# Folding a bias network's hidden rows twice by DMA, so that one last product takes 32 keys

## The chip, the core and the metric

The kernel runs on one core of a Trainium2 chip. It is one launch that computes four layers of a network, one after the other, in float32. The metric is the device time of that launch in microseconds (us). The engines have short names in the profile: PE is TensorE (matmuls) and PEld its weight loads, DVE is VectorE, ACT is ScalarE, POOL is GpSimd, SP is SyncE, which here issues DMAs. DMAs are issued by SP (plain copies) and by POOL (here all that accumulate into their target).

## The reference, cut to what matters

The change concerns layer 0 alone, an attention with a position bias that a small network computes. Per image (2) and head (8) there are 1024 queries on a 32 x 32 grid and 64 keys. For each pair of a query and a key:

```
pos  = grid_q[:, :, None, :] - grid_kv[:, None, :, :]
bias = jnp.sign(pos) * jnp.log1p(jnp.abs(pos))
bias = jax.nn.relu(bias @ cpb_w1 + cpb_b1)        # 2 -> 128
bias = jax.nn.relu(bias @ cpb_w2 + cpb_b2)        # 128 -> 128
bias = (bias @ cpb_w3 + cpb_b3)                   # 128 -> 1
sim  = q k^T + bias;  attn = softmax(sim);  out = attn v
```

The 128 x 128 product in the middle runs for 2 x 8 x 64 x 1024 pairs, about a million. Afterwards come a projection, a residual and an MLP, and then layers 1 to 3, which are further attentions on the same activations.

## The kernel before, in words

**Tiling of the bias network.** A unit u is one of the 16 (image, head) pairs. Its 64 keys are worked on in 16 quads of four keys; a quad is named by u, o (0 to 7) and half (0 or 1), and the loop in `layer0` runs over all 256 quads in this order. `first_hidden` lets DVE write the first hidden layer of the next quad: per key a tile of 128 channels x 1024 queries. `second_hidden` multiplies it, in four parts q of 32 output channels (line 704). In each part the four keys stand at four groups of 32 PSUM rows, so that four matmuls of 32 columns each run side by side; a quad has 32 matmuls, and the trace shows two records for each. ACT adds the bias, applies the ReLU and moves each part to an SBUF tile y (line 709).

**The sum over channels.** The last product, with `cpb_w3`, is a weighted sum over the 128 channels. `sorted_weights` has pulled the magnitude of each weight into the channel, and sorted the channels by the sign of the weight, so that rows which are to be added have one sign. The sum is then made of additions:

- part 0 is multiplied by a sign for each row (ACT, line 711), and added to part 1 by an accumulating DMA that POOL issues (L716);
- part 2 is added to part 3 by POOL (L720);
- one quad later, `join` adds part 1 to part 3 (POOL, L723). What remains of a quad is one tile with 32 rows for each of four keys;
- after the second quad of a pair, `join` issues two more accumulating DMAs on POOL, each 64 rows of 1024 numbers: in each of the two tiles, every second row is added to its neighbour (L725 and L726); a plain copy on SP (L727) puts the second tile's rows into the free rows of the first. Now one tile has 8 keys with 16 rows each.

**The last product.** `last_product` (L742) takes two such tiles, of 16 keys in all: four matmuls, one for each tile and each half of the queries, each with a matrix of 32 columns (`folded`) that adds up a key's 16 rows with their sign and places the key in `sim`. It stands in PE's queue four quads after the last quad of its 16 keys. When a unit's last product is done, `attend` adds the query-key product to `sim` (L768) and runs the softmax, one step a quad.

**What sets the order.** The order of PE, ACT, DVE and POOL is written out by hand (`manual_schedule`): each engine works its instructions in the order in which the loop emits them. SP works its DMAs in order as well, and waits ahead of each for what it needs. Two lists of generators, `front` (offsets, sampling and the log tables of units to come) and `after` (attention and projection of units done), are advanced by a step a quad. On SP and POOL stand also the table loads of `first_hidden`: once in four quads SP loads log positions (L620) and POOL turns them into a table tx (L622), which the first hidden layer of later quads needs. The tiles y have 2, 3, 2 and 6 buffers (tags h20 to h23).

Of the kernel before, what the change touches and what calls it, by code (L numbers as in the profile page):

```python
# [11 lines left out]
F32 = mybir.dt.float32  # L12
AF = mybir.ActivationFunctionType
ALU = mybir.AluOpType
AX = mybir.AxisListType
# [3 lines left out]
P = 128  # L19
B, C, H, W = 2, 512, 32, 32  # L20
N = H * W
CT = C // P
NB = N // P
HF = 512
DH = 64
NJ = 64
# [9 lines left out]
    ("index", 1), ("row", 1), ("sixes", 16),  # L36
# [12 lines left out]
N_FOLDED, N_SINGLE = 56, 60  # L49
# [7 lines left out]
class Net:  # L57
# [40 lines left out]
    def layer0(self):  # L98


        nc, io = self.nc, self.io
        with ExitStack() as ctx:
            keep = self.pool(ctx, "l0")
            self.l0qkv = keep.tile([P, 3, CT, P], F32, tag="qkv", name="qkv")
            x_in = io["x"].rearrange("b (t p) h w -> b t p (h w)", p=P)
            nc.scalar.dma_start(self.cols, io["cols"])
            for bt in range(BP):
                b, t = divmod(bt, CT)
# [4 lines left out]
            self.l0w2 = keep.tile([P, P], F32, tag="w2", name="w2")  # L113
# [8 lines left out]
            ow = keep.tile([P, CT, C], F32, tag="ow", name="ow")  # L122
# [8 lines left out]
            self.hid2 = self.pool(ctx, "c_hid2", 1)  # L131
            self.soft = self.pool(ctx, "c_soft", 1)
            apool = self.pool(ctx, "c_att", 1)
            ps = self.ps_h = self.pool(ctx, "c_ps_h", 3, psum=True)
# [11 lines left out]
            with self.tc.manual_schedule(engines=engines):  # L146
# [23 lines left out]
                pairs[0]["xT"] = self.fone.tile([P, NB, P], F32, tag="xnT", name="xnT00")  # L170
# [15 lines left out]
                held, self.join, self.first_z = [], None, None  # L186
                batch = []
                for i, (u, o, half) in enumerate(quads):
                    self.half = half
                    if o == 1 and half == 1 and u % 2 == 0 and u // 2 + 1 < BP:  # L190
                        nxt = pairs[u // 2 + 1]
                        front += [self.offsets(nxt, u // 2 + 1, ps), self.sampled(nxt, u // 2 + 1, ps)]
                    h1 = ready
                    if i + 1 < len(quads):
                        if quads[i + 1][1:] == (7, 0) and u + 1 < 2 * BP:
                            self.advance(front, lambda: "logs" in pairs[(u + 1) // 2])
                        ready = self.first_hidden(*quads[i + 1], pairs, tables)
                    z = self.second_hidden(u, o, half, h1, i + 1 == len(quads))
                    if half == 0:
                        batch.append((o % 2, z))  # L200
                    elif o % 2 == 1:
                        held.append((u, o, batch))
                        batch = []
                        if len(held) == 2:
                            v, last, zs = held.pop(0)
                            self.last_product(v, last, zs, sims, ps_s)
                            if last == 7:
                                if v == 8:
                                    self.advance(after, lambda: False)
                                    att = [  # L210
                                        apool.tile([P, N], F32, tag=f"att{t}", name=f"att{v}_{t}") for t in range(CT)
                                    ]
                                self.advance(front, lambda: "v" in pairs[v // 2])
                                after.append(self.attend(v, pairs[v // 2], sims.pop(v), att, ps))
                                if v % 8 == 7:
                                    after.append(self.projection(ps, att, ow, v // 8))
                    if not self.step(after):
                        self.step(front)
# [3 lines left out]
                (_, _, (ready, first)), = held  # L222
                self.last_product(u, o, [ready], sims, ps_s)
                self.single_product(u, o, 0, first[1], sims)
# [4 lines left out]
                self.single_product(u, o, 1, z, sims)  # L229
# [29 lines left out]
    def sorted_weights(self, keep):  # L259
# [7 lines left out]
        self.places = keep.tile([P, P + N_FOLDED + N_SINGLE], F32, tag="places", name="places")  # L267
        nc.scalar.dma_start(self.places, self.io["places"])
        before = keep.tile([P, P], F32, tag="before", name="before")
# [3 lines left out]
        names = ("pos", "six", "rest", "late", "gap", "neg", "first", "second", "rank", "mag", "sign")  # L273
# [8 lines left out]
        many = keep.tile([P, 16], F32, tag="many", name="sort_many")  # L282
        vec.tensor_tensor(many, self.colr("sixes", 16), total.to_broadcast([P, 16]), ALU.is_le)
        vec.tensor_reduce(c["six"], many, AX.X, ALU.add)
        vec.tensor_scalar(c["late"], c["six"], 6.0, None, ALU.mult)
        vec.tensor_scalar(c["rest"], c["six"], -6.0, 96.0, ALU.mult, ALU.add)
# [14 lines left out]
        pool.tensor_scalar(c["sign"], self.col("row"), c["six"], 2.0, ALU.is_lt, ALU.mult)  # L301
        pool.tensor_scalar(c["sign"], c["sign"], -1.0, 1.0, ALU.add, ALU.mult)
        self.folded = keep.tile([P, N_FOLDED], F32, tag="folded", name="folded")
        self.single = keep.tile([P, N_SINGLE], F32, tag="single", name="single")
        pool.tensor_scalar(self.folded, self.places[:, P : P + N_FOLDED], c["sign"], 1.0, ALU.mult, ALU.mult)
        pool.tensor_scalar(self.single, self.places[:, P + N_FOLDED :], c["sign"], 1.0, ALU.mult, ALU.mult)
        yield
        perm = keep.tile([P, P], F32, tag="perm", name="perm")
# [60 lines left out]
    def offsets(self, m, bt, ps):  # L369
# [11 lines left out]
        prod = self.fone.tile([P, 6, 6, NJ], F32, tag="prod", name=f"prod{b}{t}")  # L381
# [79 lines left out]
    def first_conv(self, qp, prod, conv, ps):  # L461
# [3 lines left out]
        diag = []  # L465
        for k in range(both, len(TAPS)):
            i = (k - both) % 8
            if i == 0:
                diag.append(self.hid2.tile([P, 8, P], F32, tag="h23", bufs=6, name=f"diag{k}"))
            nc.gpsimd.tensor_scalar(diag[-1][:, i, :], self.ident, self.col("dw_w", k), 1.0, ALU.mult, ALU.mult)  # L470
# [30 lines left out]
    def normed(self, m, bt, ahead=None):  # L501
        nc = self.nc
        b, t = divmod(bt, CT)
        if ahead:
            xn = self.hid2.tile([P, N], F32, tag="h23", bufs=6, name=f"xn{b}{t}")
        else:
            xn = self.fone.tile([P, N], F32, tag="xn", name=f"xn{b}{t}")
        m["xn"] = xn
        (ahead or nc.vector).tensor_scalar(
            xn, self.xs[b][t], self.s1[:, t : t + 1], self.col("bn1_b", t), ALU.mult, ALU.add  # L510
        )
# [30 lines left out]
    def sampled(self, m, bt, ps):  # L542
# [7 lines left out]
        if "xT" not in m:  # L550
            xT = self.fone.tile([P, NB, P], F32, tag="xnT", name=f"xnT{b}{t}")
            nc.scalar.copy(xT, self.turn(m, bt, ps))
            m["xT"] = xT
# [3 lines left out]
        w = self.fone.tile([P, NB, 2 * NJ], F32, tag="w", name=f"w{b}{t}")  # L557
# [46 lines left out]
        yield  # L604

# [85 lines left out]
    def second_hidden(self, u, o, half, h1, final):  # L691
# [6 lines left out]
        for q in range(4):  # L698
# [8 lines left out]
            y = self.hid2.tile([P, N], F32, tag=f"h2{q}", bufs=(2, 3, 2, 6)[q], name=f"h2_{u}_{o}{half}{q}")  # L707
# [14 lines left out]
        def join(final, z=ys[3], other=ys[1], first=self.first_z, fold=half == 1 and not final):  # L722
            (nc.vector if final else nc.gpsimd).tensor_tensor(z, z, other, ALU.add)  # L723
            if fold:
                nc.gpsimd.dma_start(first[0::2, :], first[1::2, :], accum_op=ALU.add)  # L725
                nc.gpsimd.dma_start(z[1::2, :], z[0::2, :], accum_op=ALU.add)  # L726
                nc.sync.dma_start(first[1::2, :], z[1::2, :])  # L727

        self.join, self.first_z = join, ys[3]
        return ys[3]  # L730

    def last_product(self, u, o, zs, sims, ps_s):

        if u not in sims:
            sims[u] = ps_s.tile([P, HF], F32, tag="sim", name=f"sim{u}")
        sim = sims[u]
        at = 24 - 4 * (o - o % 2)
        for h in range(2):  # L740
            for jj, z in zs:
                self.nc.tensor.matmul(  # L742
                    sim[h * NJ + jj * 32 : h * NJ + jj * 32 + 32, :],
                    lhsT=self.folded[:, at : at + 32],
                    rhs=z[:, h * HF : (h + 1) * HF],
                    start=(o < 2),
                    stop=False,
                )
# [1240 lines left out]
def _places():  # L1989

    q, row = np.arange(P) // 32, np.arange(P) % 32
    got = np.zeros((P, P + N_FOLDED + N_SINGLE), np.float32)
    got[:, :P] = np.where(q == 0, 96 + row, 6 * (row // 2) + 2 * (q - 1) + row % 2)
    p = np.arange(P)
    got[p, P + 24 + 4 * (p % 2) + p // 32] = 1
    got[p, P + N_FOLDED + 28 + p // 32] = 1
    return got


def _layout(i):  # L2000
# [10 lines left out]
    def over(v):  # L2011
        return np.broadcast_to(v.reshape(1, -1), (P, v.size))
# [12 lines left out]
        "row": (np.arange(P) % 32 // 2).astype(np.float32).reshape(P, 1), "sixes": over(np.arange(6, 102, 6, dtype=np.float32)),  # L2025
# [46 lines left out]
```

## Time and profile before

| | |
|---|---|
| median of 3 runs | 3251.7 us (3251.33 to 3252.86) |
| profiled execution | 3251.48 us, its span 3249.7 us |
| layer 0's loop over quads | from about 30 to about 1930 us |
| PE busy, from 100 to 1900 us | 1799.6 of 1800 us |
| POOL, ACT, DVE busy, same window | 1624, 1416, 1399 us |
| share of the 16 DMA engines busy, same window | 0.68, moving 143 GB/s |
| last product (L742), same window | 488 records, 64.4 us |
| granted PE clock | full |

The page gives busy time for each engine, then the chain of work that ended last, then groups of instructions by line. A group's row holds its count, its busy time with the mean of one in ns, and the idle time of its engine just ahead of it, with what ended most of that. Ends of matmuls are modelled, and spans on POOL are rough, so where an engine is in a steady rhythm the distance between starts says more than a duration. For a DMA the row of its line has the time that the issuing engine spends; the time from issue to landing is given apart.

### The profile page before, as it was taken

How to read it: one execution, taken by the hardware profiler on the slowest of the kernel's cores; microseconds unless marked ns; L12 is line 12 of the kernel's file. 1: busy time of each engine (PE TensorE's matmuls, PEld its weight loads, DVE VectorE, ACT ScalarE, POOL GpSimd, SP SyncE). 2: the span in 40 equal slices, each digit the busy share in tenths (PEclk: the TensorE clock that was granted, in tenths of full speed). 3: DMA queues.
4: the chain of work that ended last, by engine and by line, in shares of the span. 5: the costliest groups of instructions: out<-in, count | busy, mean ns of one | idle time of the engine just before them, and what ended most of it. 6: DMA issues, size and time to landing. Idle time of an engine off the chain costs nothing.

```text
span 3249.7 us, 59022 instructions
## 1 busy us (share of the span) xinstructions
PE 3230.7 (99%) x24436; PEld 1200.2 (37%) x24436; DVE 2388.3 (73%) x2745; ACT 1960.0 (60%) x2032; POOL 2351.6 (72%) x1563
## 2 busy tenths in 40 slices
PE   9999999999999999999999999999999999999999
PEld 4333333333333333333333334444555533455333
DVE  7877878878877677878877765575465689855897
ACT  7787887887887587887887751111131466213662
POOL 7998999999998698998999973433333458634575
PEclk9999999999999999999999999999999999999999
DMA  6676776667766566676666761111000100000001
GB/s 172 144 151 136 154 148 144 144 145 146 148 147 132 104 149 137 139 153 140 147 145 144 150 163 67 52 39 39 0 1 1 40 1 1 15 1 14 1 1 53
DMA packets 96571, 309.35 MB, mean 95 GB/s; under 512 B 14688, under 2 KB 16864, under 8 KB 93216
## 3 DMA queue, kind: packets, MB, share of 16 engines
q0 software_dynamic: 57040, 200.31, 32.6%
q1 hardware_dynamic: 38240, 103.05, 9.8%
q8 instruction: 197, 3.23, 0.4%
q10 hardware_dynamic: 1008, 2.06, 0.2%
q14 instruction: 86, 0.70, 0.1%
HBM read 67.34 MB, written 4.46 MB: 22 GB/s over the span
## 4 chain that ended last, share of the span: by engine, by line
PE 80%; POOL 11%; DVE 6%; issue 2%; ACT 1%; DMA 0%; DVEq 0%; POOLq 0%; ACTq 0%; SPq 0%
PE hp L704 41%; PE s L1610 5%; PE o L1639 5%; POOL h L723 4%; POOL h L720 4%; PE qk30P L1385 1%; PE qk20P L1385 1%; PE qk21P L1385 1%; PE m_6P L899 1%; PE m_4P L899 1%; PE m_2P L899 1%; PE m_0P L899 1%; PE qk31P L1385 1%; PE m_5P L899 1%; PE m_3P L899 1%
## 5 line engine op out<-in xcount | busy, mean ns | idle before, releaser
L704 PE MATMUL hp<-h,w2s 128*32 128x512 f32 x16384 | 1784.0, 593 | 0.5 <-DVE h L680 0.2
L680 DVE CUSTOM_DVE_ANT_1 h<-tx,bank 128x1024 f32<-128x1024 f32 (+1 forms) x1028 | 1180.4, 1211 | 299.8 <-PE hp L704 238.2
L709 ACT ACTIVATE h<-hp,magb 128x1024 f32<-128x1024 f32 x1024 | 1132.6, 1110 | 379.4 <-PE hp L704 368.7
L704 PEld LDWEIGHTS hp<-h,w2s 128*32 128x32 f32 x16384 | 531.3, 110 | 1211.9 <-issue 1184.9
L720 POOL TENSOR_TENSOR h<-h,h 128x1024 f32<-128x1024 f32 x255 | 816.6, 3203 | 1.5 <-ACT h L709 1.5
L723 POOL TENSOR_TENSOR h<-h,h 128x1024 f32<-128x1024 f32 x254 | 748.5, 2947 | 1.7 <-DMA h<-h 1.6
L716 POOL DMA_DIRECT2D h<-h x255 | 302.4, 1186 | 192.3 <-ACT h L709 179.3
L1614 ACT ACTIVATE e<-s 128x1024 f32<-128x1024 f32 x256 | 261.8, 1025 | 181.0 <-PE s L1610 175.1
L711 ACT ACTIVATE h<-h,flip 128x1024 f32<-128x1024 f32 x256 | 294.4, 1150 | 8.4
L1639 PE MATMUL o<-e,v 64*64 64x512 f32 x2048 | 265.3, 590 | 2.2 <-DVE q L1678 2.2
L1610 PE MATMUL s<-q,k 64*64 64x512 f32 x2048 | 266.0, 591 | 0.0
L1621 POOL TENSOR_TENSOR some<-some,e 128x1024 f32<-128x1024 f32 x64 | 167.6, 2619 | 26.7 <-ACT e L1614 24.2
L1619 POOL TENSOR_TENSOR some<-e,e 128x1024 f32<-128x1024 f32 x32 | 76.1, 2378 | 141.3 <-DVE sum L1628 106.3
L726 POOL DMA_DIRECT2D h<-h x127 | 175.3, 1381 | 1.0 <-issue 1.0
L725 POOL DMA_DIRECT2D h<-h x127 | 148.5, 1169 | 0.0
L1626 DVE TENSOR_TENSOR sum<-sum,e 128x1024 f32<-128x1024 f32 x64 | 123.9, 1936 | 29.9 <-ACT e L1614 26.8
L869 POOL TENSOR_TENSOR mlp_w<-mlp_w 128x512 f32<-128x512 f32 x16 | 21.2, 1325 | 164.8 <-DMA mlp_w<-in_mlp_w 140.4
L1639 PEld LDWEIGHTS o<-e,v 64*64 64x64 f32 x2048 | 77.9, 133 | 144.9 <-issue 134.8
L1610 PEld LDWEIGHTS s<-q,k 64*64 64x64 f32 x2048 | 76.6, 133 | 133.1 <-issue 117.2
L960 ACT ACTIVATE mh<-mh,cols 128x512 f32<-128x512 f32 x64 | 46.1, 721 | 124.3 <-DVE mh L978 65.4
L1373 POOL TENSOR_TENSOR sq<-q 128x512 f32<-128x512 f32 x32 | 33.2, 1039 | 99.2 <-DVE q L1392 55.1
L1624 DVE TENSOR_TENSOR sum<-e,e 128x1024 f32<-128x1024 f32 x32 | 80.8, 2524 | 32.0 <-ACT e L1614 32.0
(582 smaller groups left out, 3358.6 us busy)
## 6 DMA issues: line engine op xcount, KB each, us to landing
h<-h POOLq DMA_DIRECT2D x255, 512.0 KB, 5.4
h<-h POOLq DMA_DIRECT2D x254, 256.0 KB, 5.0
h<-h SPq DMA_DIRECT2D x127, 256.0 KB, 4.0
lb<-logs SPq DMA_DIRECT2D x63, 512.0 KB, 5.8
mlp_w<-in_mlp_w SPq DMA_DIRECT2D x16, 1024.0 KB, 5.0
x<-in_x SPq DMA_DIRECT2D x8, 512.0 KB, 7.5
qkw<-in_l_qk SPq DMA_DIRECT2D x2, 2048.0 KB, 8.0
out<-x SPq DMA_DIRECT2D x15, 256.0 KB, 2.1
```

The source lines that it names most:

```text
L680: self.nc.vector._custom_dve(TENSOR_ADD_SAT, out=h1[r][:, k, cut, :], in0=x[:, 4 * half + 2 * r + k, :].unsqueeze(1).to_broadcast([P, H // ...
L704: nc.tensor.matmul(hp[rows, cut], lhsT=self.l0w2[:, 32 * q : 32 * q + 32], rhs=h1[k][:, cut], start=True, stop=True)
L709: nc.scalar.activation(y, hp, AF.Relu, bias=self.magb[:, q, 0:1])
L711: nc.scalar.activation(y, y, AF.Copy, scale=self.flip)
L716: nc.gpsimd.dma_start(y, ys[0], accum_op=ALU.add)
L720: (nc.vector if final else nc.gpsimd).tensor_tensor(y, y, ys[2], ALU.add)
L723: (nc.vector if final else nc.gpsimd).tensor_tensor(z, z, other, ALU.add)
L726: nc.gpsimd.dma_start(z[1::2, :], z[0::2, :], accum_op=ALU.add)
L899: self.nc.tensor.matmul(acc[p], lhsT=w[:, a, k, p * P : (p + 1) * P], rhs=right(r, k), start=k == 0, stop=k == 1)
L1610: nc.tensor.matmul(s[halves[c], par, :], lhsT=ks[p][rows, at : at + DH], rhs=qs[p][rows, cut], start=True, stop=True)
L1614: nc.scalar.activation(e, s, AF.Exp, scale=DH**-0.5)
L1639: nc.tensor.matmul(o[halves[par], r, :], lhsT=v[n // 2][rows, n % 2, at : at + DH], rhs=e[rows, par, :], start=(n == 0), stop=(n == NB - 1),)
```

## The change

The tiles of part 3 of both halves of a pair become one double tile `both` of 128 rows x 2 x 1024 (three buffers). The pair is folded once by a single accumulating DMA over 64 rows of 2 x 1024, in place of L725 and L726. Two quads after the pair's second quad, the new `refold` issues a second accumulating DMA on POOL, 32 rows of 2 x 1024, after which a key has 8 rows; it stands ahead of part 3's ReLU in the program, so ahead of the L720 addition of that quad on POOL. Two plain copies on SP then gather the rows of each half, 32 rows of 1024 each, in a tile `sum` (three buffers). Two `sum` tiles hold 32 keys, and `twice_product` multiplies them in four matmuls, once in eight quads, again four quads after the last quad of the set. The last eight quads of the layer keep the single fold and the products of before, for the shorter tail.

`sorted_weights` sorts the channels so that four neighbouring rows have one sign, not two (the counts `sixes` become `twelves`); its scratch tiles, and other short-lived ones, now lie in buffers of the new tags: `spare` and `diag` in `sum`, the early `xn` in `two`; the convolution's products and the sampling's weights and image share a tile `big`. Nothing else of the kernel is changed, and the new file has new line numbers: L704 becomes L729, L716 L746, L720 L750, L723 L753, L620 L645, L622 L647. The diff, cut to its core:

```diff
-                    z = self.second_hidden(u, o, half, h1, i + 1 == len(quads))
+                    last_set = i >= len(quads) - 8
                     if half == 0:
-                        batch.append((o % 2, z))
-                    elif o % 2 == 1:
-                        held.append((u, o, batch))
-                        batch = []
-                        if len(held) == 2:
-                            v, last, zs = held.pop(0)
-                            self.last_product(v, last, zs, sims, ps_s)
...
+                        if i + 2 < len(quads):
+                            both = self.two_tiles(f"h2_{u}_{o}3")
+                            group.append([both[:, 0, :], both[:, 1, :], both])
+                        else:
+                            group.append([self.four_rows(f"h2_{u}_{o}{n}3") for n in range(2)])
+                        if o % 4 < 2 and not last_set:
+                            sums.append(self.four_rows(f"sum{u}_{o}"))
+                    self.second_hidden(i, u, o, half, h1, group[-1], i + 1 == len(quads), last_set)
+                    if half == 1 and not last_set:
+                        self.refolds.append((i + 2, group[-1][2], sums[o % 2], o % 4 // 2))
+                    if half == 1 and o % 4 == 1 and summed:
+                        v, e, zs = summed
+                        self.twice_product(v, e, zs, sims, ps_s)
+                        summed = None
...
+                    elif half == 1 and o % 4 == 3:
+                        if last_set:
+                            self.folded_product(u, o - 2, group[:2], sims)
+                        else:
+                            summed, group, sums = (u, o // 4, sums), [], []
...
@@ second_hidden
-            y = self.hid2.tile([P, N], F32, tag=f"h2{q}", bufs=(2, 3, 2, 6)[q], name=f"h2_{u}_{o}{half}{q}")
+            if q < 3:
+                y = self.hid2.tile([P, N], F32, tag=f"h2{q}", bufs=(2, 3, 2)[q], name=f"h2_{u}_{o}{half}{q}")
+            else:
+                y = one[half]
+                if self.refolds and self.refolds[0][0] <= i:
+                    self.refold(*self.refolds.pop(0)[1:])
...
             if fold:
-                nc.gpsimd.dma_start(first[0::2, :], first[1::2, :], accum_op=ALU.add)
-                nc.gpsimd.dma_start(z[1::2, :], z[0::2, :], accum_op=ALU.add)
-                nc.sync.dma_start(first[1::2, :], z[1::2, :])
+                nc.gpsimd.dma_start(one[2][0::2], one[2][1::2], accum_op=ALU.add)
+                if last_set:
+                    nc.sync.dma_start(one[0][1::2, :], one[1][0::2, :])
...
+    def refold(self, both, to, second):
+        nc = self.nc
+        nc.gpsimd.dma_start(both[0::4], both[2::4], accum_op=ALU.add)
+        for half in range(2):
+            nc.sync.dma_start(to[2 * second + half :: 4, :], both[0::4, half, :])
+
+    def twice_product(self, u, e, zs, sims, ps_s):
+        if u not in sims:
+            sims[u] = ps_s.tile([P, HF], F32, tag="sim", name=f"sim{u}")
+        at = 16 - 16 * e
+        self.sum_product(u, self.twice[:, at : at + 32], e == 0, zs, sims)
...
+    def four_rows(self, name):
+        return self.hid2.tile([P, N], F32, tag="sum", bufs=3, name=name)
+
+    def two_tiles(self, name):
+        return self.hid2.tile([P, 2, N], F32, tag="two", bufs=3, name=name)
```

## The prediction

> **What bounds the kernel now.** I read the page's first part, then its chain, then the groups, and last the timeline around the products that the change touches.
>
> ```profile
> PE 3230.7 (99%) x24436; PEld 1200.2 (37%) x24436; DVE 2388.3 (73%) x2745; ACT 1960.0 (60%) x2032; POOL 2351.6 (72%) x1563
> ...
> PE 80%; POOL 11%; DVE 6%; issue 2%; ACT 1%; DMA 0%; DVEq 0%; POOLq 0%; ACTq 0%; SPq 0%
> ...
> L704 PE MATMUL hp<-h,w2s 128*32 128x512 f32 x16384 | 1784.0, 593 | 0.5 <-DVE h L680 0.2
> ...
> L720 POOL TENSOR_TENSOR h<-h,h 128x1024 f32<-128x1024 f32 x255 | 816.6, 3203 | 1.5 <-ACT h L709 1.5
> L723 POOL TENSOR_TENSOR h<-h,h 128x1024 f32<-128x1024 f32 x254 | 748.5, 2947 | 1.7 <-DMA h<-h 1.6
> L716 POOL DMA_DIRECT2D h<-h x255 | 302.4, 1186 | 192.3 <-ACT h L709 179.3
> ...
> L726 POOL DMA_DIRECT2D h<-h x127 | 175.3, 1381 | 1.0 <-issue 1.0
> L725 POOL DMA_DIRECT2D h<-h x127 | 148.5, 1169 | 0.0
> ```
>
> PE is never idle, and its 16,384 hidden-layer records waited 0.5 us in all. The 99% alone proves little, because ends of matmuls are modelled; the timeline of PE, cut to two lines, proves it:
>
> ```profile
> 607.13 13.92 PE L704 MATMUL hp<-h,w2s 128*32 128x512 f32 x128
> ...
> 634.94 1.04 PE L742 MATMUL sim<-h,folded 128*32 128x512 f32 x8
> ```
>
> 128 records (two quads) take 13.87 us wherever the chain shows them as one piece, so eight records take 13.87 x 8 / 128 = 0.867 us, without a gap. Layer 0's time is the sum of its matmuls, and a product on L742, eight records, costs 0.867 us (its shown 1.04 includes a modelled tail: the one at 606.27 was followed by the next quad at 607.13, 0.86 later).
>
> **What the Trainium skill says.** Trace Analysis (its opening note) calls matmul busy time a bad metric since matmuls are pipelined; hence the spacing above. TensorEngine Tiling, Key Properties: column tiles run independently and in parallel. The trace agrees: a record lasts 593 ns, and eight pass in 867. DMA: Bandwidth & Descriptors, Anatomy of one DMA: DMA engines do not wait on semaphores, the issuing sequencer does; so a copy that is not ready blocks everything behind it on SP. The same page, SDMA does more than copy: an accumulate handles at most 2048 elements; the new fold's rows are exactly 2 x 1024, the old ones 1024. No run here shows yet how such a row goes.
>
> **The change part by part.**
>
> *Products.* Before: 63 full products of four matmuls, and two lone matmuls of L742 at the end. After: 31 products of 32 keys, one folded product for half of the last set, and the same two lone matmuls. The two built programs' counts, 254 and 130 matmuls, agree: 124 go, that is 31 products. 31 x 0.867 = 26.9 us. All stood on PE in order, with nothing to hide them.
>
> *POOL.* Per two quads the issues were L716 twice, L725, L726; they are now L716 twice, one fold (64 rows x 8 KB), one refold (32 rows x 8 KB). The same number, so nothing, but the refold moves to the odd quad, before its L720, and now waits for the fold to land. POOL's real spacing is below its rough spans:
>
> ```profile
> 615.75 1.17 POOL L725 DMA_DIRECT2D h<-h  x1
> 616.41 1.39 POOL L726 DMA_DIRECT2D h<-h  x1
> 616.99 3.23 POOL L720 TENSOR_TENSOR h<-h,h 128x1024 f32<-128x1024 f32 x1
> 619.37 1.58 POOL L622 TENSOR_SCALAR tx<-lb,cols 128x512 f32<-128x512 f32 x1
> ...
> 623.04 3.53 POOL L720 TENSOR_TENSOR h<-h,h 128x1024 f32<-128x1024 f32 x1
> ```
>
> An issue holds it about 0.6 us, an addition 2.35. From a fold to its refold POOL does an issue, L720, L716, L723: 0.6 + 2.35 + 0.6 + 2.35 = 5.9 us, 6.6 with L622. Two 256 KB accumulates issued together land as
>
> ```profile
> DMA to landing us min/median/max: 4.2/5.3/9.1
> ```
>
> (L726); the first was issued 0.65 earlier, so the fold, as many bytes in one, should land 5.3 to 6 us after its issue. The refold waits 0 to 0.7 us; I take 0.3. Behind it stand L720 and then L716, for which ACT waits only when two quads later its buffer is still held. POOL's cover is its wait for ACT ahead of L716: 173.5 us in the window from 100 to 1900 us, 5.6 us per 8 quads (some 58 us each), less 0.9 for the shorter quads.
>
> *DMA.* Per pair 256 KB more are accumulated (768 for 512); the plain copies keep 256 KB, in two. The window's queue line prices it:
>
> ```profile
> q0 software_dynamic: 54293, 190.63, 56.0%
> ```
>
> 56% of 1800 us for 190.6 MB is 5.3 us per MB with all engines; 124 pairs x 0.262 MB add 32.5 MB, 172 us, spread over some 1850: the busy share of 0.68 becomes about 0.77. That is no limit, but landings may lengthen by some tenths.
>
> *SP.* The copies of one refold now stand ahead of the next load of log tables (L620), which L622 on POOL reads. In the shown stretch L620 was issued at 611.65. It would now wait for the refold at 608.8 (the slot of L720 there) to land, 5.0 later, and for two issues of 0.47: 614.8. Its own median landing is 5.8, so L622 starts at 620.6 for 619.37. Done so for the 31 sets, with the refold landing in 4.6, 5.0 or 5.4, POOL loses 0.5, 0.8 or 1.1 us on average (at most 2.3) each four quads. With the refold waits: 4 x 0.3 + 2 x 0.8 = 2.8 us per 8 quads, under the cover of 4.7.
>
> *The product's own wait.* This is the term that can cost. The last refold of a set stands in the second quad before the product. In the timeline its slot is 623.04 and the product's weights start at 634.94 - 0.43 = 634.51: 11.5 us. Over the 31 products that remain, this distance is 10.5 to 12.5 us, mean 11.9 with one outlier of 19. Into it must go: L622's delay (0.8), the refold's landing (5.0, between L725's median 4.6 and L726's 5.3), 0.1 for SP, 0.47 for a second issue, and a copy's landing:
>
> ```profile
> DMA to landing us min/median/max: 2.2/4.0/6.2
> ```
>
> (L727, 256 KB; each new copy has half of that). 0.8 + 5.0 + 0.1 + 0.5 + 4.0 = 10.4: 1.5 us to spare. Set by set, with 4.6, 5.0, 5.4 for the refold, 0, 2 and 6 of the 31 are late, by 0, 0.6 and 3.4 us in sum. Landings scatter around their medians, so I take 1.5 us. With copies at half length (say 3.0, by the smaller size) it would be nothing.
>
> *The rest.* The double tiles, sums and the scratch they replace occupy released buffers; ACT's write into a double tile needs copies that were issued more than two quads earlier: nothing. The shared tile for convolution products and sampling is used by steps already in sequence on the front list, one a quad: nothing; if a step waited, one DVE operation of 1.2 us would, under DVE's 286 us of waits. The set-up sort compares with 8 numbers for 16 and makes one sign tile for two: less than 1 us either way. The tail keeps its length (one 512 KB fold for two of 256).
>
> Sum, against the profiled execution's 3251.5 (span 3249.7 and 1.8 around it): 3251.5 - 26.9 + 1.5 = 3226.1. The median of runs, 3251.7, is 0.2 above.
>
> **The rivals.** What a measurement can tell from no change is about 0.2%, 6.5 us.
>
> *Products wait in part.* The refold lands like the slower half of L726 and the chain takes a further 0.4 to 0.8 us: 31 x 0.15 to 0.6 = 5 to 19 us lost, 3230 to 3243. For it: only 1.5 us to spare, a busier DMA. Against: copies of half the size.
>
> *Slower: the product as the new bound.* Place: the first matmul of each 32-key product. 31 waits of s cost 31 s; the gain is gone at s = 0.87 us, and it is measurably slower from 1.08 on, when the chain from refold slot to last copy exceeds 11.9 + 1.1 = 13.0 us rather than 10.4. If 2048-element rows accumulated so slowly that a refold took 8.5 us (L725's longest), the chain would be 13.9, s = 2.0, and the time 3225 + 62 = 3287. It repeats, since POOL's pace follows ACT and PE. For it: rows of that length are nowhere in this trace. Against: bytes, not rows, set the landing between L716 (512 KB, 5.4) and L725 (256 KB, 4.6).
>
> *POOL becomes the bound.* With every refold waiting 0.7 and each L622 1.9, 6.6 us per 8 quads, over the cover of 4.7: 31 x 1.9 = 59 us, 3284. Against: these are worst cases taken together; it decides from 4.7 us per 8 quads, 2.8 are expected.
>
> *The change doesn't do what it says:* excluded, since 124 matmuls are gone from the built program.
>
> **How the numbers follow.** Products in time, 3222 to 3230: 0.58. Waiting in part, 3230 to 3245: 0.24. Gain eaten up, within 0.2% of before: 0.07. Slower by either mechanism: 0.11. So faster 0.82, same 0.07, slower 0.11. The range of 8 in 10 is 3221 to 3246: the first two cases; 3221 is the product term with 4 us for landings and waits that get shorter. Where it is faster, 3223 to 3232 is the likeliest case's own range.
>
> **What would show it.** PE: 31 x 8 records fewer on L742's successor, the spacing of eight quads from 57.4 to 56.5, and idle before the product's row near nothing, against tens of us for the slow rival (released by DMA). POOL: idle before the refold and before L622's successor of about 0.3 and 0.8 us, released by DMA; idle ahead of the L716 row falling from 192 to some 80 to 130. Landings: fold 5.3 to 6, refold near 5, copies 3 to 4. DMA share near 0.77. The prediction is wrong if fold or refold rows of 8 KB land above 8 us, or if PE's idle shows up at rows that had none.

## The result and the profile after

| | before | after |
|---|---|---|
| median of 9 runs | 3251.43 us (3250.18 to 3252.89) | 3243.97 us (3239.92 to 3249.37) |
| profiled execution, span | 3251.48, 3249.7 us | 3249.37, 3247.6 us |
| first to last hidden-layer record (the loop) | 1900.61 us | 1890.17 us |
| last hidden-layer record to the MLP's first matmul (the tail) | 34.01 us | 41.46 us |
| from there to the end | 1291.94 us | 1292.80 us |

The ratio is 0.9979, with an interval of 0.997 to 0.9987. The kernel is faster by 7.5 us where 25.4 were forecast, and its runs scatter over 9.5 us for 2.7 before.

The products are gone as counted: 260 records at L785 for 508 at L742. A stretch of eight quads in which nothing else happens took 57.38 us before and takes 56.52 after, 0.86 less; at 0.858 each the 31 products are 26.6 us. Yet the loop became only 10.4 us shorter: 16.2 us were lost in it. The tail grew by 7.5 and the rest by 0.9 (this last is scatter: over all the runs below it took 1290.0 to 1293.3). So -26.6 + 16.2 + 7.5 + 0.9 = -2.0 for a span that shrank by 2.1. (This profiled execution is the slowest of the nine; the median keeps 5 us more.)

The page of the kernel after, in the order of the lines shown of before: busy time by engine, the chain, and the groups. L755 issues the fold, L765 the refold; L785 holds the products.

```profile
PE 3223.4 (99%) x24188; PEld 1221.3 (38%) x24188; DVE 2427.2 (75%) x2745; ACT 1960.6 (60%) x2032; POOL 2355.6 (73%) x1559
...
PE 84%; DVE 10%; POOL 4%; issue 2%; ACT 1%; DMA 1%; DVEq 0%; POOLq 0%; ACTq 0%; SPq 0%
...
L729 PE MATMUL hp<-h,w2s 128*32 128x512 f32 x16384 | 1795.2, 592 | 2.1 <-DVE h L705 1.0
...
L753 POOL TENSOR_TENSOR h<-h,h 128x1024 f32<-128x1024 f32 x254 | 723.9, 2850 | 0.0
L750 POOL TENSOR_TENSOR h<-h,h 128x1024 f32<-128x1024 f32 x255 | 718.7, 2818 | 1.5 <-ACT h L739 1.5
...
L746 POOL DMA_DIRECT2D h<-h x255 | 269.7, 1058 | 119.9 <-ACT h L739 116.3
...
L765 POOL DMA_DIRECT2D h<-h x124 | 141.5, 1141 | 21.0 <-DMA h<-h 19.2
...
L755 POOL DMA_DIRECT2D h<-h x127 | 109.1, 859 | 39.0 <-POOL h L753 37.2
```

PE's idle ahead of its hidden-layer records grew from 0.5 to 2.1 us. That row cannot hold 16 lost microseconds: they show only in the distance between starts, because ends of matmuls are modelled and can close gaps in the record. The distances say where they are. Of 255 steps from quad to quad most differ by less than 0.12 us from before (the product apart); in the units 3, 5, 7 and 13 three steps are longer by 0.44, 2.48 and 0.82, together 3.75 us a unit. That is 15 of the 16.2 (other steps lose 4.1; before had a loss of 2.9 of its own in unit 10, which is gone). In these units DVE's groups, cut to the two lines that differ, read before

```profile
L441 DVE TENSOR_TENSOR log<-log,pos 128x64 f32<-128x64 f32 x7 | 6.4, 919 | 0.0
L419 DVE TENSOR_TENSOR pos<-grid,at 128x64 f32<-128x64 f32 x7 | 4.4, 632 | 0.2
```

and after

```profile
L451 DVE TENSOR_TENSOR log<-log,pos 128x64 f32<-128x64 f32 x7 | 36.3, 5183 | 0.0
L429 DVE TENSOR_TENSOR pos<-grid,at 128x64 f32<-128x64 f32 x7 | 21.5, 3065 | 0.2
```

Both are multiplications or subtractions of 64 numbers a partition, once for a pair of units, in the generator that prepares the log tables; the diff doesn't touch them. L451 (`log*sign`) is the worst: 2.1, 7.2, 7.2, 6.9, 1.4, 4.3 and 7.2 us one by one, against 0.75 to 1.38 before. The four long ones belong to the four units that lose 3.75 us. The timelines around one of them show how. Columns are start, duration, engine, line. DVE and POOL before:

```profile
415.51 0.84 DVE L441 TENSOR_TENSOR log<-log,pos 128x64 f32<-128x64 f32 x1
417.25 4.61 DVE L680 CUSTOM_DVE_ANT_1 h<-tx,bank 128x1024 f32<-128x1024 f32 x4 [0.90 <-PE hp L704]
...
413.02 3.24 POOL L720 TENSOR_TENSOR h<-h,h 128x1024 f32<-128x1024 f32 x1
415.42 1.57 POOL L622 TENSOR_SCALAR tx<-lb,cols 128x512 f32<-128x512 f32 x1
416.14 1.70 POOL L716 DMA_DIRECT2D h<-h  x1
416.77 3.49 POOL L723 TENSOR_TENSOR h<-h,h 128x1024 f32<-128x1024 f32 x1
```

and after:

```profile
413.24 7.17 DVE L451 TENSOR_TENSOR log<-log,pos 128x64 f32<-128x64 f32 x1
420.33 4.60 DVE L705 CUSTOM_DVE_ANT_1 h<-tx,bank 128x1024 f32<-128x1024 f32 x4
...
410.39 2.68 POOL L750 TENSOR_TENSOR h<-h,h 128x1024 f32<-128x1024 f32 x1
412.79 1.02 POOL L647 TENSOR_SCALAR tx<-lb,cols 128x512 f32<-128x512 f32 x1
413.51 1.15 POOL L746 DMA_DIRECT2D h<-h  x1
414.13 2.95 POOL L753 TENSOR_TENSOR h<-h,h 128x1024 f32<-128x1024 f32 x1
416.54 1.34 POOL L765 DMA_DIRECT2D h<-h  x1
417.14 3.17 POOL L750 TENSOR_TENSOR h<-h,h 128x1024 f32<-128x1024 f32 x1
419.94 1.21 POOL L746 DMA_DIRECT2D h<-h  x1
...
421.68 18.53 PE L729 MATMUL hp<-h,w2s 128*32 128x512 f32 x146 [0.26 <-DVE h L705]
```

Before, `log*sign` came while POOL's addition L720 had 0.75 us to run, and ended 0.09 us behind the end of it. After, it came 0.17 us behind the end of the same addition (now L750). It then took as long as L647, L746, L753, L765 and the next L750 together, and ended 0.10 us behind the end of that L750. DVE's next first hidden layer began with no wait at all, where before it had 0.90 us to spare, and PE waited for it.

The other records fit. This instruction stands on DVE with both operands in SBUF in before, after and, below, e1, e6 and e10: 35 times in all, and every time it ended 0.09 or 0.10 us behind the recorded end of an addition on POOL. The 20 that came at least 0.45 us ahead of the end of L720 or L750 ended there. The 15 that came between 0.21 us ahead of this end and 0.52 us behind it did not. Of these, eight ended behind L753, after 3.6 to 4.3 us, where the next instruction on POOL started 2.75 us or more behind L753's start; seven had to wait for the next L750, 6.9 to 7.2 us, where it started after 2.73 us or less. So in unit 11 above: L765 had to wait for its fold's DMA, and started 3.01 us after L753 rather than 2.41; that `log*sign` ended at 4.3 us, right there.

The Trainium skill (SBUF — State Buffer, section SBUF: two separate sides) describes a lock: VectorE and GpSimd share a pair of SBUF ports, a DVE operation with two inputs in SBUF needs it, and whichever engine starts first "gets the pair for the whole instruction". The trace agrees in that DVE waits for POOL to end an instruction, but one instruction does not explain 7.17 us: here DVE was kept out through several that followed each other without a pause.

The tail has another cause. PE in the tail of after:

```profile
1937.41 0.69 PE L855 MATMUL bank<-pt,v 64*64 64x256 f32 x2 [4.28 <-DVE pt L844]
...
1938.47 9.67 PE L255 MATMUL ob<-att,ow 128*128 128x512 f32 x16
```

and DVE there:

```profile
1923.55 0.17 DVE L95 TENSOR_SCALAR bn2s<-cols 128x4 f32<-128x4 f32 x1 [5.87 <-PE sim L796]
1923.75 1.00 DVE L976 TENSOR_SCALAR mx<-x,bn2s,cols 128x512 f32<-128x512 f32 x2
```

The same 16 matmuls on PE and the same first instruction of the MLP on DVE, before:

```profile
1943.91 7.13 PE L246 MATMUL ob<-att,ow 128*128 128x512 f32 x16
...
1925.54 0.15 DVE L95 TENSOR_SCALAR bn2s<-cols 128x4 f32<-128x4 f32 x1
```

The MLP's first tiles (`bn2s`, `mx`) have nothing to do with the bias network. Now DVE waited 5.87 us for the last product to make them; before, it made them without a wait, 1.8 us after the loop's end for 10.2 now. So they stand between the last softmax's steps, PE waits 4.28 us for its `pt`, and its granted clock stands at half for 6.8 us from 1936.8 on, so that the same 16 matmuls on L255 took 9.67 us for 7.13. (The Trainium skill, TensorE: Matmul & The Clock Gate, Part 1, states that the array falls to half clock after an idle window of about 3.4 us. The trace agrees: the clock fell 3.7 us into the wait. The stretch at half clock is 6.8 us here, and 3.4 or 6.8 us in e7 below.) The products read tiles of the pool `c_hid2`. The change opens this pool right behind layer 0's first pool; before, other pools came ahead of it. If the MLP's first pool lies over what the last product still reads, that explains the wait.

### The profile page after: what moved, and what is told of

Same layout as the page of the kernel before. It is cut to its first block, busy times and chain, and to the rows that moved or that the text cites. A ratio compares the mean times of both kernels' runs of the same rounds, so it can differ in the third digit from the quotient of the medians.

```text
span 3247.6 us, 58820 instructions
## 1 busy us (share of the span) xinstructions
PE 3223.4 (99%) x24188; PEld 1221.3 (38%) x24188; DVE 2427.2 (75%) x2745; ACT 1960.6 (60%) x2032; POOL 2355.6 (73%) x1559
## 4 chain that ended last, share of the span: by engine, by line
PE 84%; DVE 10%; POOL 4%; issue 2%; ACT 1%; DMA 1%; DVEq 0%; POOLq 0%; ACTq 0%; SPq 0%
PE hp L729 46%; PE s L1653 5%; PE o L1682 5%; DVE h L705 3%; PE qk20P L1428 1%; PE qk30P L1428 1%; PE m_5P L942 1%; PE m_3P L942 1%; PE m_2P L942 1%; PE m_0P L942 1%; PE qk31P L1428 1%; PE qk21P L1428 1%; PE m_6P L942 1%; PE m_4P L942 1%; PE m_1P L942 1%
## 5 line engine op out<-in xcount | busy, mean ns | idle before, releaser
L729 PE MATMUL hp<-h,w2s 128*32 128x512 f32 x16384 | 1795.2, 592 | 2.1 <-DVE h L705 1.0
L729 PEld LDWEIGHTS hp<-h,w2s 128*32 128x32 f32 x16384 | 558.6, 110 | 1200.2 <-issue 1123.7
L753 POOL TENSOR_TENSOR h<-h,h 128x1024 f32<-128x1024 f32 x254 | 723.9, 2850 | 0.0
L750 POOL TENSOR_TENSOR h<-h,h 128x1024 f32<-128x1024 f32 x255 | 718.7, 2818 | 1.5 <-ACT h L739 1.5
L1657 ACT ACTIVATE e<-s 128x1024 f32<-128x1024 f32 x256 | 261.8, 1024 | 181.1 <-PE s L1653 177.2
L746 POOL DMA_DIRECT2D h<-h x255 | 269.7, 1058 | 119.9 <-ACT h L739 116.3
L765 POOL DMA_DIRECT2D h<-h x124 | 141.5, 1141 | 21.0 <-DMA h<-h 19.2
L755 POOL DMA_DIRECT2D h<-h x127 | 109.1, 859 | 39.0 <-POOL h L753 37.2
```

Of the source, the lines that this page charges most:

```text
L729: nc.tensor.matmul(hp[rows, cut], lhsT=self.l0w2[:, 32 * q : 32 * q + 32], rhs=h1[k][:, cut], start=True, stop=True)
L746: nc.gpsimd.dma_start(y, ys[0], accum_op=ALU.add)
L750: (nc.vector if final else nc.gpsimd).tensor_tensor(y, y, ys[2], ALU.add)
L1657: nc.scalar.activation(e, s, AF.Exp, scale=DH**-0.5)
```

## The experiments

Three theories were to be told apart. **Port**: DVE instructions with two SBUF operands are shut out by POOL. **Order**: the place of the pool makes the MLP wait. **Late products**: the forecast's first rival, in which products wait for their copies. The kernel before, run on the same chips, took 3250.71 us (e1 to e4), 3250.86 (e5 to e8) and 3252.1 (e9, e10), so medians of different sets compare to some 1.4 us. All edits are to the kernel after, unless said otherwise.

**e1_order: pools in another order, nothing else.**

```diff
             keep = self.pool(ctx, "l0")
+            self.fpool = self.pool(ctx, "f", 2)
+            self.fone = self.pool(ctx, "f1", 1)
+            self.lpool = self.pool(ctx, "c_log", 2)
+            self.tab = self.pool(ctx, "c_tab", 2)
+            self.hid = self.pool(ctx, "c_hid", 4)
             self.hid2 = self.pool(ctx, "c_hid2", 1)
...
-            (the same five lines, from further down)
```

> The changed kernel, with the SBUF pool of the double tiles and sums opened after the layer's other pools again, so that the MLP's first tiles no longer lie where the last tiles of layer 0 lie. Theory (two losses: a tail of 7.5 us by placement, 16 us in the loop by DVE's waits for POOL): the first MLP matmul comes 34 us after the last hidden record, as before the change, not 41.5; time 3240 (3238 to 3242), with less scatter than the changed kernel's 9 us. Rival (the tail was long because PE's clock happened to drop): the distance stays above 38 us in this profile or the median stays at 3244.

Measured: 3239.69 us (3233.66 to 3246.08), ratio 0.9968 (0.9956 to 0.998). The tail is back at 34.16 us, with no half-clock stretch in it; the loop is still long (1888.9), and `log*sign` still took 32.3 us in seven. The order of opening pools is the tail's cause. The scatter, forecast to shrink, stayed (12 us in six runs), so the tail is not its source.

**e2_psum: the second operands in PSUM.** The offsets `at` and the sign go to columns of a PSUM bank that is already there, so neither instruction has two operands in SBUF.

```diff
-        at = self.fpool.tile([P, 2], F32, tag="at", name=f"at{b}{t}")
+        at = self.bank[:, 448:450] if bt else self.fpool.tile([P, 2], F32, tag="at", name=f"at{b}{t}")
...
-            nc.scalar.activation(pos, pos, AF.Sign)
+            sign = self.bank[:, 384:448].rearrange("p (d x) -> p d x", d=2)
+            nc.scalar.activation(sign, pos, AF.Sign)
...
-            nc.vector.tensor_tensor(log, log, pos, ALU.mult)
+            nc.vector.tensor_tensor(log, log, sign, ALU.mult)
```

> The changed kernel, with two small operands of the offset steps (the offsets, and the sign of the positions) held in PSUM, so that no DVE instruction there reads two SBUF operands. Theory (DVE's product log x sign waits for the SBUF port that POOL holds): that row falls from a mean of 5.2 us to below 0.5, the offset rows of 3 us too; PE loses 1 to 4 us in the loop rather than 16; time 3231 (3228 to 3235), the tail unchanged. Rival (DVE is slow there because of the heavier DMA traffic or of POOL being late): the row stays at 3 to 7 us whatever memory its operand is in, and the time stays near 3244.

Measured: 3233.19 us (3232.63 to 3235.51), ratio 0.9947 (0.9933 to 0.996). DVE's groups:

```profile
L452 DVE TENSOR_TENSOR log<-log,bank 128x64 f32<-128x64 f32 x7 | 1.5, 211 | 0.0
L429 DVE TENSOR_TENSOR pos<-grid,bank 128x64 f32<-128x64 f32 x7 | 1.5, 220 | 0.2
```

`log*sign` itself costs 0.21 us; all the rest of its 5.18 was waiting. It did not merely come at a better time: in all seven cases an addition of POOL was running when it came, and ran on for 1.8 us or more behind that. The loop took 1877.4 us, so the loss in it fell from 16.2 to 3.4, and the runs scatter over 2.9 us for 9.5. The tail stayed at 41.15. So DVE's wait for POOL, which the second operand in SBUF brings, is the cause of the loop's loss. That what it waits for is a port is not shown; the runs show only that the operand's place decides. The scatter may have the same cause, but five runs are few (those of e3 scatter over 5.9 us).

**e3_both: both edits.**

> Both edits together on the changed kernel. Theory: the losses add, so the time is 3251.4 - 26.9 + 1 to 4: 3226 (3224 to 3230). Rival (a third cause, products or POOL): above 3233.

Measured: 3228.51 us (3225.68 to 3231.55), ratio 0.9932 (0.9918 to 0.9946); loop 1879.0, tail 34.16. The two causes add up: 4.3 us (e1) and 10.8 (e2) against the median after, 15.5 together. This is the lowest median of the study, 2.4 us above the forecast.

**e4_before_psum: the edit of e2 in the kernel before.**

> The kernel before with the PSUM operands alone. Theory: there the same instructions met a free port (0.9 us for log x sign; offsets 3.05 in some units), and PE lost 3 us at most, so 3248 to 3251.4. Rival (the operands' place is worth 13 us on any kernel): 3238.

Measured: 3255.25 us (3253.89 to 3256.69), ratio 1.0014 (1.0007 to 1.002): slower by 4.5 us, which no theory had. `log*sign` took 0.21 us here as well, so a wait that had not made PE late gave nothing back, and the edit has a price of its own. The loop is 3.9 us longer, by 0.40 to 0.85 us at quad 8, 9 or 12 of each odd unit up to 13. Of e3's rest of 5 us in the loop only 0.85 us lie at such a quad (12 of unit 9), and the kernel after, without the edit, loses 0.63 there.

**e5_order_sign and e8_before_sign: the sign alone in PSUM**, in e1 and in the kernel before (the last two hunks of e2).

> The changed kernel with the pool order restored and the sign alone held in PSUM (the offsets stay in SBUF). The loop of the run with both edits was 1879.0 us, and the kernel before with both operands in PSUM was 4.5 us slower than before, 3.9 of it in the loop, so one of the two operands costs something by itself. If the offsets' place costs it: loop 1874 to 1877 us, time 3224 to 3226, with log x sign at 0.2 us. If the sign's place costs it: as the run with both, 3228.5.

> The kernel before with the sign alone in PSUM. If the offsets' place was what cost 4.5 us there: 3250 to 3251.5, as before. If the sign's place was: 3255.

Measured: e5 3229.77 us (3228.11 to 3232.59), ratio 0.9937 (0.9923 to 0.995); e8 3255.41 us (3253.43 to 3257.22), ratio 1.0013 (1.0006 to 1.0019). So the sign does it, for good and ill. The offsets' row shows what a wait is worth that has slack behind it; in e5:

```profile
L429 DVE TENSOR_TENSOR pos<-grid,at 128x64 f32<-128x64 f32 x7 | 21.5, 3071 | 0.2
```

The subtraction still lost 2.85 us each time, seven times, and the loop (1879.9) is within 1 us of e3's. It stands at another place of the quad. Where the sign's price in the kernel before arises, the waits of e8 tell:

```profile
DVE h L681 <- ACT bank L437: 18.2, 6, 5.3
```

(A line of the waits gives their sum, their number and the longest.) L437 is the Sign activation. The bank that was chosen for the sign is the tile `bank`, which DVE's first hidden layer (L681) reads; so this layer now waits for ACT's sign, as it never did before. The price is then one of this bank, not of PSUM. That is argued: a sign in another bank was not tried.

**e6_order_gap: one more instruction on POOL, a copy of one column**, after L753 in the quads without a fold, ahead of the refold. It waits for that addition and so makes a gap.

```diff
             if fold:
...
+            elif not final:
+                nc.gpsimd.tensor_copy(self.tick, z[:, 0:1])
```

> The changed kernel with the pool order restored, all operands in SBUF as changed, and one tiny POOL copy of a 128x1 column ahead of each refold, which reads what the L753 addition just wrote, so that POOL has to wait for its own addition there. It adds work to POOL and takes none away. Theory (DVE's product waits until POOL's run of additions has a gap): log x sign is at most 4.3 us instead of 7.2, the loop's loss against the products' 26.9 us falls from 14.9 to about 5, time 3229 to 3234. Rival (DVE waits because POOL is too busy or late): the added POOL work leaves the row at 7 us and the time at 3240 or above.

Measured: 3234.21 us (3230.37 to 3237.14), ratio 0.995 (0.9936 to 0.9963): 5.5 us below e1, with more work on POOL. The ranges of the two overlap; the loops of the profiled executions, 1883.2 us for e1's 1888.9, say the same. DVE and POOL:

```profile
414.29 3.62 DVE L452 TENSOR_TENSOR log<-log,pos 128x64 f32<-128x64 f32 x1
417.83 4.60 DVE L706 CUSTOM_DVE_ANT_1 h<-tx,bank 128x1024 f32<-128x1024 f32 x4
...
413.52 1.01 POOL L648 TENSOR_SCALAR tx<-lb,cols 128x512 f32<-128x512 f32 x1
414.24 1.15 POOL L747 DMA_DIRECT2D h<-h  x1
414.87 2.95 POOL L754 TENSOR_TENSOR h<-h,h 128x1024 f32<-128x1024 f32 x1
417.88 0.18 POOL L760 COPY tick<-h 128x1 f32<-128x1 f32 x1
418.13 0.85 POOL L768 DMA_DIRECT2D h<-h  x1
```

`log*sign` came even later behind the table (0.77 us), and ended where the gap opens. All five that had taken 3.7 to 7.2 in e1 took 3.58 to 3.62. The later arrival is not the reason: in unit 11 of e1 it came 0.78 us behind the table, found no gap, and took 6.86. The lack of a gap in POOL's run is what makes 7 us out of 3.6.

**e9_order_pool and e10_order_later: away from the port, or at another time.** e9 lets POOL do `log*sign` (`nc.gpsimd.tensor_tensor(log, log, pos, ALU.mult)`); e10 puts one more `yield` after the Sign activation, so that DVE does it a step of the quad loop later.

> The changed kernel with the pool order restored, and the product log x sign made by POOL instead of DVE, operands in SBUF. DVE then never waits for the port there, and the sign needs no PSUM, whose place cost 4.5 us on the kernel before. POOL gets some 0.3 us of work in each of 7 units. Theory: loop 1875 to 1880 us, time 3224 to 3229. Rival (POOL has no room): the loop stays at 1885 or above, time 3235 or more.

> The changed kernel with the pool order restored, and DVE's product log x sign one step, so one quad, later, in a quad in which POOL has a fold and with it a gap; nothing else is moved but the steps behind it. Theory (POOL's run of additions without a gap in the other quads is the cause): log x sign at most 3.7 us in all units, the loop's loss below 9 us, time 3228 to 3234. Rival (the row is slow in any quad since the change): 5 to 7 us again, 3239.

Measured: e9 3230.39 us (3227.18 to 3231.48), ratio 0.9932 (0.9918 to 0.9946), loop 1879.2. That is some 1.5 us over the expected range; its ratio is that of e3, without an operand in PSUM. e10 3236.32 us (3229.63 to 3236.43), ratio 0.9951 (0.9937 to 0.9964): in the profiled execution (3229.63, the fastest of its five) the instruction took 0.55 to 2.6 us, ending behind L751 all seven times, and the loop 1879.9, as expected. The median is above what was expected, so the new place seems not to be safe in every run; the slower ones have no profile.

**e7_late_refold: e3 with the refold three quads after its fold, not two** (`self.refolds.append((i + 3, ...`). It measures the forecast's rival: what late products would have cost.

> Both mended edits (pool order, offsets and sign in PSUM), and each refold one quad later. It tests the cover of the product's wait: in the changed kernel refolds land 3.7 us after their issue and copies 3.3 us after theirs, so some 3.5 to 4 us are to spare. One quad later is 7 us, and the refold then stands directly behind a fold on the queue, 1 to 2 us more. Theory (the product is the next bound, and every wait is paid by PE in full): 4 to 5 us at each of 31 products, 3350 to 3385. If other engines' slack took it: 3228 to 3235.

Measured: 3447.26 us (3445.49 to 3460.09), ratio 1.0615 (1.0597 to 1.0634): more than the 3350 to 3385 expected. The waits for the products' input, and PE's timeline at one of them:

```profile
PE sim L786 <- DMA sum<-h: 115.3, 26, 6.8
```

```profile
633.70 0.96 PE L786 MATMUL sim<-sum,signed 128*32 128x512 f32 x3 [3.81 <-DMA sum<-h]
```

The loop lost 224 us, 7.2 for each of the 31 products where 4 to 5 were expected: 4 to 8 in the product's quad and some 2 us more in the quad behind it, where PE's clock stood at half for 3.4 or 6.8 us after nearly every one (29 stretches). So a product that waits is plainly seen as "DMA sum", and the quad behind it loses some 2 us more at half clock. In the kernel after, the same view gives

```profile
PEld sim L785 <- DMA sum<-h: 1.1, 3, 0.4
```

and the 31 steps that hold its products (quads 3 and 11 of the units) are as long as before, to 0.01 us. This settles it: the products were not late.

## Why the prediction failed

**Right.** *The change doesn't do what it says* was rightly excluded, and a product costs the 0.867 us that the spacing gave (0.86 measured). *The product's own wait*, taken as 1.5 us, was 1.1 (from 100 to 1880 us); the refold stood 10.6 us ahead of its product (8.5 to 12.1, one outlier of 17.7 left out) where 11.9 less 0.8 was counted. *Products wait in part* and *the product as the new bound* did not happen, and the measured 3244 next to the 3230 to 3243 of the former is no evidence for it. That it lies inside the whole range, 3221 to 3246, is luck: that range was made of waits for DMAs. Rows of 8 KB accumulate without harm: the fold landed in 4.4 / 5.8 / 9.3 us (min / median / max; 5.3 to 6 forecast), the refold in 3.7 for 5.0, the copies in

```profile
sum<-h SPq DMA_DIRECT2D x248, 128.0 KB, 3.3
```

3.3 us (DMA issues; median from issue to landing) for 4.0. The DMA share is 0.77, as worked out. The refold's wait for its fold came to 18.9 us in 24 of 121, half of the 0.3 us each that was taken; ahead of L647, for which SP's copies were to cost 0.8 us each, POOL did not wait at all. It did wait 39 us ahead of L755 for its own L753, which no term had. POOL's cover ahead of L746 fell from 192 to 120 us, inside the 80 to 130; *POOL becomes the bound* did not happen.

**Wrong: "The rest".** It said that if a step of the shared list waited, "one DVE operation of 1.2 us would, under DVE's 286 us of waits", hence nothing. The term is 16.2 us in the profiled execution. It failed twice. The estimate looked only at buffers as a reason to wait, and a step that the diff doesn't touch, `log*sign`, waits for POOL because both its operands are in SBUF: after the change it came 0.17 us behind the end of a POOL addition, into a run without a gap, where before it came 0.75 us ahead of that end. And the 286 us of DVE's waits are a sum: at this place DVE had 0.90 us until the next first hidden layer, and needed 6.3 more.

**Wrong: "*POOL.* … The same number, so nothing".** The number of issues is indeed the same, and POOL isn't the bound. But it was priced by POOL's own time alone. L765 follows L753 at once when its fold has landed, which the forecast counted as the good case. It is the case in which DVE stays shut out; the refold that waits lets DVE in (4.3 us in unit 11). e6 shows it: one more instruction, with a gap ahead of the refold, and the loop is 5.8 us shorter than e1's.

**Wrong: "The tail keeps its length".** It grew by 7.5 us, of which e1 gave back 7.3 in the profiled executions and 4.3 in the medians. The forecast counted the tail's DMAs; it didn't ask what the new order of pools puts under the next layer's first tiles. The diff moves that line, but the prediction didn't cost it. That tiles lie over each other is inferred from the wait on PE and from e1; addresses were not looked at.

**The signs.** "Idle near nothing" at the products' rows was right and reassured wrongly: the loss appears in no PE row. The spacing of quads, used for the product's price, would have been the sign to name for the losses as well.

**What stays open.** The products' 26.6 us off 3251.4 make 3224.8; the best kernel has 3228.5. These 4 us lie in scattered quads (2.0 us at quad 3 of unit 14, 0.85 at quad 12 of unit 9 in e3's profile). They are not the price of the sign's bank alone: e9, without it, has a loss of 5.2 us in its loop too, 1.4 of it at the same quad of unit 14. Open as well is why DVE is let in behind L750 with no pause on POOL's record, and behind L753 only with one; and which part of the change moved `log*sign` from 0.75 us ahead of an addition's end to 0.17 behind it.

## What to carry to other kernels

Where PE is the bound and work is taken off it, look at what the shorter rhythm does to engines that have slack on average: a DVE instruction with two SBUF operands beside a POOL that works without a gap can take 7 us for 0.2, and a wait removed on POOL can be what let it in. An operand that is moved to PSUM to escape this can bring a new wait, if others read its bank. Look for rows whose mean is far above that of the same operation with other operands, and measure losses by the distance between starts. When a change opens a pool earlier, ask which tiles of the next layer will lie over it, and what reads these last.

## What the runs showed of the hardware

- A 128x64 multiplication on DVE took 0.21 us with one operand in PSUM, an addition of POOL running beside it, and 0.55 to 7.19 us with both in SBUF. With both in SBUF it ended 0.09 or 0.10 us behind the end of a POOL addition, 35 times of 35. Where it missed one, it was let in behind the next (3.6 to 4.3 us) if POOL's following instruction came 2.75 us or more behind that addition's start, and one addition later (6.9 to 7.2 us) if it came after 2.73 us or less.
- Waits of PE of some 4 us and more were followed by half its clock for 3.4 or 6.8 us (the tail of after; 29 stretches in e7's loop): some 2 us more per wait in e7.
- An accumulating DMA from SBUF to SBUF with rows of 2048 numbers lands like one of 1024: 256 KB in 3.7 us (median) for 5.0 before, where two were issued together, and 512 KB in 5.8, for 5.4 to 5.5 with rows of 1024.
